# A decoder layer on one core: other queues for three early loads, a second bank for one early product, and two Pool sequences moved by two places and one

## The chip, the core and the metric

The kernel runs on one core of one Trainium2 chip. Five engines matter: TensorE (PE in the profile, its weight loads PEld), VectorE (DVE), ScalarE (ACT), GpSimd (POOL) and SyncE (SP). SP, ACT and POOL can issue DMAs; the profile calls their issuing sides SPq, ACTq and POOLq, and the queues of packets q1 (SP's), q10 (ACT's) and q0 (POOL's). The metric is the device time of one execution in microseconds; less is better. Before the change the median of three runs is 2976.89 us (2976.18 to 2977.85).

## The reference

One decoder layer in float32 over 32 x 64 = 2048 token rows of 512 features. Only the first stage is touched by the change:

```python
q = (x @ wq.T).reshape(b, l, NH, HD)          # 32 heads of 128
k = (x @ wk.T).reshape(b, l, NKV, HD)         # 8 key heads
v = (x @ wv.T).reshape(b, l, NKV, HD)
q, k = apply_rope(q, ...), apply_rope(k, ...)
k_full = concatenate([k_cache[block_idx].reshape(-1, NKV, HD), k[0]])   # 512 cached rows + 64 new
v_full = concatenate([v_cache[block_idx].reshape(-1, NKV, HD), v[0]])
attn = softmax(q @ k_full.T / sqrt(HD))
x = layernorm(x + (attn @ v_full) @ wo.T)
```

After it come cross attention over a second input of the same size, a feed-forward part with eight low-rank experts, and a layer norm after each. They are the same before and after.

## The kernel before, in words

**Tiling.** The 2048 rows are four token blocks of 512 (`NTB`), the 32 query heads are eight groups of four (`g`), each group with its own key head. A unit `n` is one head of one token block: 128 units, four to a block `b`, 16 to a group. In unit `n` PE computes scores (`scores`, L865 to L897), DVE takes the row maximum, ACT the exponentials, DVE turns the weights with a 32x32 transpose, SP moves them with sixteen DMAs (`move`, L933) into `pT`, and PE multiplies them with the values two units later (`values`, L954). PE fills the rest of a unit with products of the query projection for the next block and of the output projection for earlier ones.

**Products.** A 512x512x512 projection is done as seven half-size products (a Strassen-Winograd scheme). `Product.mul` (L374) is one of them: eight matmuls into one PSUM bank. The operands are quarters of the weights and tokens, and sums and differences of quarters. For the first block the query product numbered 1 uses `wq0[1]` and token quarter `q[0,0]`; number 2 uses `wq0[2]` and `q[1,0]`; number 5 uses `wq0[5]`, which is first `wq0[5] + wq0[4]` made by DVE (L1215), and `t[1]` (L1213); number 6 uses `wq0[6]` (L1217) and `t[2]` (L1216). `Queries.step(1)` (L405) writes product 1 to bank `x` and lets ACT copy it to the query tile (L409). `step(2)` accumulates product 2 onto the same bank `x`, so it must come behind that copy, and ACT copies the sum (L413).

**The order of the start** (L718 to L1261) is written by hand for all five engines. SP issues the block indices, three token quarters and weight quarter `wq0[5]`, the rotary tables `cs` and `sn` (L736), the key and value weights of group 0 (`load_group(0, nc.sync)`, L1191, issued at L761), four small vectors, the tokens of block 1 (L116) and four quarters of the output weights. ACT issues three weight quarters and the fourth token quarter `q[1,1]`. POOL writes `off_i` (L742), gathers four times 128 cached key rows (L772), copies the 64 new tokens out of the token quarters (`x128`, L1209), helps with the rotation of the cached keys (`rotate`, L795), and gathers the values. DVE makes operands, rotates the keys in two halves (L1218, L1220), prepares a scale `nrm2` (L1221 to L1224) and adds products up (L1237, L1238, L1246). PE does products 1, 2, 5, 6 of block 0, the new keys and values (`new_keys`, L818: eight matmuls with `wk`, eight with `wv`), the transposes of the rotated keys (`cached_keys`, L842, into the bank `s0`, one half of a scores tile called `startbank`), product 3, and then the first scores.

HW-issued DMAs (SP's and ACT's together) share eight completion semaphores in turn, so the ninth such DMA is issued only when the first has landed; POOL's DMAs have eight of their own. That is why an issue on SP can wait for an older load of SP or ACT.

**Tokens' sums.** Later blocks use a deeper scheme whose token operands are prepared once per token block by POOL: `token_leaves(tb)` (L1078) is a list of 20 steps with places 0 to 19: four loads of 256 KB from `xD` (places 0 to 3, two DMAs each, L1089 and L1090), sums (L1094) and stores to DRAM (L1098). A place is a quarter of a unit: place `p` runs at `n = 1 + p // 4`, quarter `p % 4` (`leaf`, L1407). The line `place += (16, 36, 54, 72)[tb]` (L1273) gives the start of the four sequences. All four use one tile `tq`. At each place without a store POOL also issues one held-back load (`spread`).

Of the kernel before, what the change touches and what calls it, by code (L numbers as in the profile page):

```python
# [9 lines left out]
F32 = mybir.dt.float32  # L10
I32 = mybir.dt.int32
AF = mybir.ActivationFunctionType
ALU = mybir.AluOpType
# [3 lines left out]
P = 128  # L17
# [35 lines left out]
def decoder_layer(  # L53
# [32 lines left out]
    nc = tc.nc  # L86
# [45 lines left out]
    special = {}  # L132

    def bank(shape, name, tag=None):
        if tag in special:
            v = special[tag]
            return v.rearrange("p (a b) -> p a b", a=shape[1])
        return psum[-1].tile(shape, F32, tag=tag or "ps", name=name)
# [105 lines left out]
    def quarter(i, j):  # L244

        return slice(2 * i, 2 * i + 2), slice(j * HF, (j + 1) * HF)
# [20 lines left out]
    def load_quarter(dst, src, i, j, queue=nc.sync):  # L267
        r = slice(i * HF, (i + 1) * HF)
        queue.dma_start(
            out=dst, in_=src[r, j * HF : (j + 1) * HF].rearrange("(c p) n -> p c n", p=P)  # L270
        )
# [48 lines left out]
    def load_right_first(src, name, queue=nc.sync, held=None):  # L320
        w = {}
        load_some(src, name, w, ((1, (0, 0)), (2, (1, 0))), queue, held)
        return w
# [384 lines left out]
    with ExitStack() as ph:  # L708
# [3 lines left out]
        sc = ph.enter_context(tc.tile_pool(name="sc", bufs=2, space=PSUM))  # L712
# [10 lines left out]
        NKT = NSEL // P  # L723
# [4 lines left out]
        q = {(i, j): xTs[0][:, quarter(i, j)[0], quarter(i, j)[1]]  # L728
             for i in range(2) for j in range(2)}
        for i, j, n, (k, m) in ((0, 0, 1, (0, 0)), (1, 0, 2, (1, 0)), (0, 1, 5, (0, 1)), (1, 1, 4, (1, 1))):  # L730
            load_quarter(q[i, j], xT_in, i, j, (nc.sync, nc.scalar)[i and j])
            load_quarter(wq0[n], wqT[:, : REP * HD], k, m, (nc.scalar, nc.sync)[n == 5])
        cs = kc.tile([P, HD // 2], F32, name="cs")
        sn = kc.tile([P, HD // 2], F32, name="sn")
# [6 lines left out]
        for i in range(P // BLOCK):  # L741
            nc.gpsimd.iota(  # L742
                off_i[i * BLOCK : (i + 1) * BLOCK, :], pattern=[[0, 1]], base=0,
                channel_multiplier=1,
            )
        off = kc.tile([P, 1], F32, name="off")
        nc.vector.tensor_copy(off, off_i)
        nc.vector.tensor_scalar(off, off, float(NKV), None, ALU.mult)
# [8 lines left out]
        def load_group(g, queue=nc.scalar):  # L757
            ws = []
            for tag, src in (("wk", wkT), ("wv", wvT)):
                w = kv.tile([P, NC, HD], F32, tag=tag, name=f"{tag}{g}", bufs=1)  # L760
                load = lambda w=w, src=src: queue.dma_start(  # L761
                    out=w, in_=src[:, g * HD : (g + 1) * HD].rearrange("(c p) n -> p c n", p=P)
                )
                if g == 0:
                    load()
                else:
                    spread.append(load)
                ws.append(w)
            wkv_cur[g] = ws
# [25 lines left out]
        def rotate(g, t0=0, t1=NKT):  # L795


            kn = kn_cur[g][:, t0:t1, :].rearrange("p t (d two) -> p t d two", two=2)
            k4 = kr_cur[g][:, t0:t1, :].rearrange("p t (d two) -> p t d two", two=2)
            shape = [P, t1 - t0, HD // 2]  # L800
            c3 = cs[:, None, :].to_broadcast(shape)
            s3 = sn[:, None, :].to_broadcast(shape)
            tmp = kv.tile(shape, F32, tag="tmp", name=f"kt{g}_{t0}", bufs=1)
            tmq = kv.tile(shape, F32, tag="tmq", name=f"kq{g}_{t0}", bufs=1)
            e, o = kn[:, :, :, 0], kn[:, :, :, 1]
            nc.gpsimd.tensor_tensor(k4[:, :, :, 1], o, c3, ALU.mult)
            nc.vector.tensor_tensor(tmq, e, s3, ALU.mult)
            nc.vector.tensor_tensor(k4[:, :, :, 0], e, c3, ALU.mult)
            nc.vector.tensor_tensor(tmp, o, s3, ALU.mult)
            nc.gpsimd.tensor_tensor(k4[:, :, :, 1], k4[:, :, :, 1], tmq, ALU.subtract)  # L810
            nc.vector.tensor_tensor(k4[:, :, :, 0], k4[:, :, :, 0], tmp, ALU.add)
# [6 lines left out]
        def new_keys(g):  # L818

            wk, wv = wkv_cur.pop(g)
            kTs[g] = kv.tile([P, NKEY], F32, tag="kT", name=f"kT{g}")
            new = bank([P, 1, TB], f"new{g}", "po1")[:, 0, :]
            pk, pv = new[:, :SEQ], new[:, P : 2 * P]
            for c in range(NC):
                nc.tensor.matmul(
                    pk, wk[:, c, :], x64[:, c, :], start=(c == 0), stop=(c == NC - 1),
                    skip_group_check=True,
                )  # L830
            for c in range(NC):
                nc.tensor.matmul(
                    pv, x128[:, c, :], wv[:, c, :],
                    start=False, stop=(c == NC - 1), skip_group_check=True,
                )
            nc.scalar.activation(
                kTs[g].rearrange("p (s b k) -> p s b k", s=2, k=SQ)[:, :, SHARED, :],
                pk.rearrange("p (s k) -> p s k", s=2), AF.Copy, scale=nrm2,
            )
            nc.scalar.copy(vs[g][:, NKT, :], pv)  # L840
# [148 lines left out]
        def columns(g):  # L989
            return slice(g * REP * HD, (g + 1) * REP * HD)  # L990

        def start_queries(b, tags):
            g, tb, _ = units[b * REP]
            qTs[b] = big.tile([P, REP, TB], F32, tag="qT", name=f"qT{g}_{tb}", bufs=2)
            qrs[b] = Queries(wq_cur[g], tok.pop(b), qTs[b], f"q{g}_{tb}", tags)
# [192 lines left out]
                    for v, d in ((1, d1), (2, d5), (0, d7)):  # L1188
                        g.tensor_tensor(q[:, v, :, :], q[:, v, :, :], d, add)  # L1189

        load_group(0, nc.sync)  # L1191
        cs2 = kc.tile([P, 1], F32, name="cs2")
        sn2 = kc.tile([P, 1], F32, name="sn2")
        for dst, src in ((cs2, cos2), (sn2, sin2)):
# [4 lines left out]
        xTs[1] = token_room(1, "xT1")  # L1199
        load_features(xTs[1], xT_in, 1)  # L1200
        wo_cur[0] = load_right_first(woT[columns(0), :], "wo0")
        special["s0"] = sc.tile([P, 2, 512], F32, tag="sc", name="startbank")[:, 0, :]

        sub = ALU.subtract
        t = {i: txs[:, i - 1, :, :] for i in range(1, 5)}
# [11 lines left out]
        nc.vector.tensor_tensor(wq0[6], wq0[5], wq0[1], sub)  # L1217
        rotate(0, 0, NKT // 2)  # L1218
        nc.vector.tensor_tensor(wq0[3], wq0[2], wq0[6], sub)
        rotate(0, NKT // 2, NKT)  # L1220
        nc.vector.tensor_tensor(nrm2, cs2, cs2, ALU.mult)  # L1221
        nc.vector.tensor_tensor(sn2, sn2, sn2, ALU.mult)
        nc.vector.tensor_tensor(nrm2, nrm2, sn2, ALU.add)
        nc.vector.tensor_scalar(nrm2, nrm2, SCALE, None, ALU.mult)  # L1224
        wq_cur[0] = wq0
        tok[0] = {1: q[0, 0], 2: q[1, 0], 3: q[1, 1], 4: t[4], 5: t[1], 6: t[2], 7: t[3]}
        start_queries(0, {"x": "q", "y": "w", "z": "po0"})


        first = qrs[0]  # L1230
        c = first.c
        first.step(1)
        first.step(2)
        z = first.mul("z", 5, True)
        y = first.mul("y", 6, True)
        new_keys(0)
        nc.vector.tensor_tensor(c[1, 1], z, c[1, 0], ALU.add)  # L1237
        nc.vector.tensor_tensor(c[0, 1], y, c[1, 0], ALU.add)  # L1238
        nc.vector.tensor_tensor(t[3], q[1, 1], q[0, 1], sub)
        for j in range(NKT):  # L1240
# [29 lines left out]
        leaves, full = {}, set()  # L1270
        for tb in range(NTB):
            for place, part in token_leaves(tb):
                place += (16, 36, 54, 72)[tb]  # L1273
                leaves.setdefault(place, []).append(part)
                if part.__name__ == "store":
                    full.add(place)
# [3 lines left out]
        for n in range(N):  # L1280
# [6 lines left out]
            if 0 < n <= PER:  # L1287
                b2, j = divmod(n - 1, TPB)
# [246 lines left out]
    with ExitStack() as ph:  # L1535
# [39 lines left out]
        def run(todo, count=None):  # L1575
            for _ in range(len(todo) if count is None else min(count, len(todo))):
                todo.pop(0)()
# [37 lines left out]
        with ExitStack() as st:  # L1615
# [8 lines left out]
            def add_bias(tb, j):  # L1624
                a = acc[tb][:, j, :]
                nc.vector.tensor_tensor(a, a, bo, ALU.add)
# [11 lines left out]
            def place(step, todo):  # L1638

                while step in fill:  # L1640
                    step += 1
                fill[step] = todo
                return step + 1
# [14 lines left out]
            for k, tb in enumerate((1, 2, 3, 0)):  # L1658
                stats, (head, *pieces) = layernorm_parts(tb, "a", by_act=True)
                i = place(17 * k, lambda stats=stats: run(stats, 2))  # L1660
                i = place(i, lambda stats=stats: run(stats))
                i = place(i + 1, head)
# [14 lines left out]
            i = 0  # L1677
            for tb, last in zip((1, 2, 3, 0), turned_at):
                i = max(i, last + 2)
                for j in range(TPB):  # L1680
                    while i in fill or i - 1 in fill and i + 1 in fill:
                        i += 1
                    i = place(i, lambda tb=tb, j=j: add_bias(tb, j)) + 1
# [62 lines left out]
        sc = ph.enter_context(tc.tile_pool(name="xsc", bufs=2, space=PSUM, reuse_waits="tile"))  # L1746
# [519 lines left out]
```

## Time and profile before

| what | value |
|---|---|
| median of three runs | 2976.89 us (2976.18 to 2977.85) |
| profiled execution, its own time | 2975.92 us |
| span of that execution | 2974.1 us |
| PE busy | 2953.5 us (99%) |
| DVE, ACT, POOL busy | 1907.9, 1481.7, 1699.0 us |
| PE's first matmul | 5.52 us |
| first product of block 0 on PE | 5.52 to 9.27 us |
| second product | 9.94 to 13.5 us |
| third product | from 13.52 us |
| first scores | 20.96 us |

All times are from the start of the span. The program is one long chain on PE; what lies outside of PE counts only where PE waits. In the timeline an entry reads: start, duration, engine, line, operation, output <- inputs, count, and in brackets the idle time before it with what ended it.

### The profile page before, as it was taken

The page shows a single profiled execution, that of the slowest core. Times are in us where ns is not written, and L with a number is a line of the kernel's source. Part 1 is how long each engine was busy: PE and PEld are TensorE (multiplying, and loading weights), DVE is VectorE, ACT ScalarE, POOL GpSimd, SP SyncE. Part 2 cuts the span into 40 slices and gives each one's busy share as a digit, 9 for nine tenths or more (in the row PEclk, how much of TensorE's full clock was granted, in tenths as well). Part 3 has the DMA queues.
Part 4 walks back from the last instruction along what each step waited for, and adds up shares of the span by engine and source line. Part 5 has one row for each costly group of instructions (what it writes and reads, how often), then busy time and mean ns, then how long its engine had stood idle before and what let it go on. Part 6 is the DMA issues. An engine that isn't in the chain of part 4 may idle for free.

```text
span 2974.1 us, 49389 instructions
## 1 busy us (share of the span) xinstructions
PE 2953.5 (99%) x17152; PEld 2336.2 (79%) x17152; DVE 1907.9 (64%) x3568; ACT 1481.7 (50%) x3304; POOL 1699.0 (57%) x1697
## 2 busy tenths in 40 slices
PE   9999999999999999999999999999999999999998
PEld 6677777777777777777777768999999999999965
DVE  6766666666666666666666665636666666666676
ACT  5444455555455455555555552334555555555564
POOL 5666654564564564664663534658577577567532
PEclk9999999999999999999999999999999999999999
DMA  6677656666666666665566554766455445445420
GB/s 171 182 200 196 171 143 157 159 162 158 156 166 157 154 166 157 154 168 154 155 168 156 136 132 147 255 234 214 160 185 184 168 168 194 166 162 184 137 82 36
DMA packets 220454, 487.31 MB, mean 164 GB/s; under 512 B 52912, under 2 KB 88112, under 8 KB 212016
## 3 DMA queue, kind: packets, MB, share of 16 engines
q1 hardware_dynamic: 177872, 341.51, 39.6%
q0 software_dynamic: 40672, 140.68, 16.7%
q8 instruction: 139, 2.28, 0.3%
q10 hardware_dynamic: 1664, 1.97, 0.2%
q14 instruction: 107, 0.88, 0.1%
HBM read 264.27 MB, written 46.66 MB: 105 GB/s over the span
## 4 chain that ended last, share of the span: by engine, by line
PE 96%; DVE 1%; DMA 1%; SPq 1%; ACT 1%; issue 0%; POOL 0%; POOLq 0%; DVEq 0%
PE po L949 17%; PE s L875 16%; PE qd L1168 9%; PE sx L1762 2%; PE pox L1845 2%; PE qx_0x L519 2%; PE qx_1x L519 2%; PE qx_2x L519 2%; PE qx_3x L519 2%; PE wx_3y L380 1%; PE wx_2y L380 1%; PE wx_0y L380 1%; PE w_3y L380 1%; PE w_0y L380 1%; PE w_2y L380 1%; PE wx_1y L380 1%
## 5 line engine op out<-in xcount | busy, mean ns | idle before, releaser
L875 PE MATMUL s<-kT,qT 128*128 128x288 f32 x2048 | 581.3, 408 | 0.0
L888 ACT ACTIVATE p<-s,nmax 128x576 f32<-128x576 f32 x512 | 378.4, 739 | 362.7 <-DVE nmax L882 341.2
L949 PE MATMUL po<-pT,v 128*128 128x512 f32 (+1 forms) x1280 | 549.5, 603 | 4.6 <-DMA pT<-T 4.2
L882 DVE TENSOR_REDUCE nmax<-s 128x1 f32<-128x576 f32 x512 | 384.5, 751 | 249.1 <-PE s L875 244.2
L919 ACT ACTIVATE p<-p,den 128x576 f32<-128x576 f32 x416 | 322.8, 776 | 354.6 <-DVE den L917 352.8
L875 PEld LDWEIGHTS s<-kT,qT 128*128 128x128 f32 x2048 | 371.0, 190 | 107.2 <-issue 33.9
L929 DVE STREAM_TRANSPOSE T<-p 128x576 f32<-128x576 f32 x512 | 395.6, 773 | 45.7 <-ACT p L919 41.0
L1145 POOL DMA_DIRECT2D tq<-tq x336 | 182.8, 547 | 417.2 <-PE qd L1168 403.4
L949 PEld LDWEIGHTS po<-pT,v 128*128 128x128 f32 (+1 forms) x1280 | 204.0, 189 | 191.0 <-issue 175.4
L1168 PEld LDWEIGHTS qd<-tq,wq 128*128 128x128 f32 x1344 | 174.5, 191 | 48.4 <-issue 31.8
L1168 PE MATMUL qd<-tq,wq 128*128 128x128 f32 x1344 | 179.0, 276 | 0.0
L1168 PEld LDWEIGHTS qd<-tq,xT 128*128 128x128 f32 x1008 | 136.3, 191 | 51.9 <-issue 23.0
L1168 PE MATMUL qd<-tq,xT 128*128 128x128 f32 x1008 | 142.1, 277 | 0.0
L1865 ACT ACTIVATE oTx<-pox,bv 128x128 f32<-128x128 f32 x248 | 71.3, 490 | 128.3 <-PE pox L1845 128.3
L917 DVE RECIPROCAL den<-den 128x1 f32<-128x1 f32 x512 | 78.5, 153 | 72.2 <-ACT p L888 70.7
L1189 POOL TENSOR_TENSOR qT<-qT,tx 128x512 f32<-128x512 f32 x72 | 89.2, 1267 | 61.5 <-DVE qT L1177 61.4
L351 POOL TENSOR_TENSOR sox<-oTx,oTx 128x512 f32<-128x512 f32 x31 | 39.3, 1268 | 148.1 <-DVE oTx L1867 144.3
L1794 ACT ACTIVATE exps<-exps,denx 128x64 f32<-128x64 f32 x480 | 121.1, 338 | 0.0
L561 POOL TENSOR_TENSOR qTx<-d_in 128x512 f32<-128x512 f32 x68 | 85.2, 1275 | 34.5 <-ACT d_in L537 26.7
L888 ACT ACTIVATION_READ_ACCUMULATOR p<-s,nmax 128x1 f32 x512 | 99.5, 194 | 0.0
L1175 ACT COPY tx<-qd 128x512 f32<-128x512 f32 x96 | 56.1, 584 | 67.2 <-PE qd L1168 62.3
L561 POOL TENSOR_TENSOR qTx<-d 128x512 f32<-128x512 f32 x60 | 75.1, 1275 | 25.0 <-ACT d L537 23.5
(626 smaller groups left out, 6352.3 us busy)
## 6 DMA issues: line engine op xcount, KB each, us to landing
pT<-T SPq DMA_DIRECT2D x1016, 80.0 KB
pT<-T SPq DMA_DIRECT2D x1008, 64.0 KB
xT<-tl SPq DMA_DIRECT2D x28, 1792.0 KB
tq<-tq POOLq DMA_DIRECT2D x168, 256.0 KB
tlb<-tl SPq DMA_DIRECT2D x28, 1344.0 KB
tq<-tq POOLq DMA_DIRECT2D x168, 192.0 KB
kv_room<-kv SPq DMA_DIRECT2D x32, 512.0 KB
pTx<-Tx SPq DMA_DIRECT2D x256, 64.0 KB
```

The lines of the kernel that those rows point to most:

```text
L380: nc.tensor.matmul(self.banks[b][:, m, :], self.left[i][:, k, m * P : (m + 1) * P], self.right[i][:, k, :], start=(first and m + k == 0), ...
L519: nc.tensor.matmul(o[:, j, :], self.left[s][:, j, LEFT[i], :], self.right[s][:, j, RIGHT[i], :], start=(first and j == 0), stop=(j == len( ...
L561: nc.gpsimd.tensor_tensor(self.q[:, :, i, :, v, :], x.rearrange("p (o u) n -> p o u n", o=2), y.rearrange("p (o u) n -> p o u n", o=2), AL ...
L875: nc.tensor.matmul(s[:, a, :HALF], query_block(n, i), kTs[g][:, a * HALF : (a + 1) * HALF], start=True, stop=True,)
L882: nc.vector.tensor_reduce(nmax, s[:, :, :HALF], AX.XY, ALU.max, negate=True)
L888: nc.scalar.activation(p.rearrange("q (a k) -> q a k", a=2), s[:, :, :HALF], AF.Exp, bias=nmax, accum_out=den,)
L919: nc.scalar.activation(p, p, AF.Copy, scale=den)
L929: nc.vector.transpose(Ts[n][:, :, i, :], ps_.pop((n, i)).rearrange("q (b k) -> q b k", k=SQ))
L949: nc.tensor.matmul(pos[n].rearrange("d (a q) -> d a q", a=NQD), vs[units[n][0]][rows, v, :], pTs[n // 2][rows, :, chunk, :], skip_group_ch ...
L1145: nc.gpsimd.dma_start(out=tq[:, r, : 4 - s, :], in_=tq_all[b % NTB][:, r, 4 * s : 4 + 3 * s, :],)
L1168: nc.tensor.matmul(o[:, j, :], wdeep[s][:, j, LEFT[i], :], tq[:, RIGHT[i], j, :], start=(first and j == 0), stop=(j == js - 1), skip_group ...
L1794: nc.scalar.activation(e[:, k, :], e[:, k, :], AF.Copy, scale=den[:, k : k + 1])
```

## The change

1. The token quarter `q[1,1]` is no longer issued by ACT between two weight quarters; POOL issues it behind `off_i`, ahead of the key gathers.
2. The key and value weights of group 0 are no longer issued by SP behind the rotary tables; ACT issues them behind its copy of product 1.
3. Product 2 has a PSUM bank of its own, the second half of `startbank` (`s1`), and no longer accumulates onto bank `x`. ACT's copy of the sum is gone; DVE adds bank `s1` and the copy of product 1 instead.
4. The rotation of the second half of the cached keys is done by DVE and POOL behind the four `nrm2` operations, in program order behind `new_keys`.
5. The token sums of block 1 start at place 38 instead of 36, those of block 2 at place 55 instead of 54.

```diff
         for i, j, n, (k, m) in ((0, 0, 1, (0, 0)), (1, 0, 2, (1, 0)), (0, 1, 5, (0, 1)), (1, 1, 4, (1, 1))):
-            load_quarter(q[i, j], xT_in, i, j, (nc.sync, nc.scalar)[i and j])
+            if (i, j) != (1, 1):
+                load_quarter(q[i, j], xT_in, i, j)
             load_quarter(wq0[n], wqT[:, : REP * HD], k, m, (nc.scalar, nc.sync)[n == 5])
...
                 channel_multiplier=1,
             )
+        load_quarter(q[1, 1], xT_in, 1, 1, nc.gpsimd)
         off = kc.tile([P, 1], F32, name="off")
...
-        load_group(0, nc.sync)
         cs2 = kc.tile([P, 1], F32, name="cs2")
...
-        special["s0"] = sc.tile([P, 2, 512], F32, tag="sc", name="startbank")[:, 0, :]
+        startbank = sc.tile([P, 2, 512], F32, tag="sc", name="startbank")
+        special["s0"], special["s1"] = startbank[:, 0, :], startbank[:, 1, :]
...
         rotate(0, 0, NKT // 2)
         nc.vector.tensor_tensor(wq0[3], wq0[2], wq0[6], sub)
-        rotate(0, NKT // 2, NKT)
         nc.vector.tensor_tensor(nrm2, cs2, cs2, ALU.mult)
...
-        start_queries(0, {"x": "q", "y": "w", "z": "po0"})
+        start_queries(0, {"x": "q", "y": "w", "z": "po0", "2": "s1"})
...
         first.step(1)
-        first.step(2)
+        load_group(0, nc.scalar)
+        second = first.mul("2", 2, True)
         z = first.mul("z", 5, True)
         y = first.mul("y", 6, True)
         new_keys(0)
+        rotate(0, NKT // 2, NKT)
         nc.vector.tensor_tensor(c[1, 1], z, c[1, 0], ALU.add)
+        nc.vector.tensor_tensor(c[0, 0], second, c[1, 0], ALU.add)
         nc.vector.tensor_tensor(c[0, 1], y, c[1, 0], ALU.add)
...
-                place += (16, 36, 54, 72)[tb]
+                place += (16, 38, 55, 72)[tb]
```

## The prediction, made before the result was known

> **What bounds the kernel now.** I read the page first, then PE's waits over the whole span, then chain, timeline and waits of the first 26 us, because the change lies there but for one line.
>
> ```profile
> span 2974.1 us, 49389 instructions
> PE 2953.5 (99%) x17152; PEld 2336.2 (79%) x17152; DVE 1907.9 (64%) x3568; ACT 1481.7 (50%) x3304; POOL 1699.0 (57%) x1697
> ```
>
> PE is busy 2953.5 of 2974.1 us. The 20.6 us left are all that better waiting can win.
>
> ```profile
> engine line waited for: us in total, times, longest us
> PE q_0x L380 <- DMA xT<-in_xT: 5.5, 1, 5.5
> PE po L949 <- DMA pT<-T: 4.2, 5, 1.3
> PE q_0x L380 <- ACT qT L409: 0.7, 1, 0.7
> ```
>
> PE's waits: 5.5 us for the first tokens, 4.2 us in five waits for moved weights, and 0.7 us between products 1 and 2, the wait for ACT's copy that the change removes.
>
> ```profile
> 9.94 3.76 PE L380 MATMUL q_0x<-xT,wq 128*128 128x256 f32 x8 [0.68 <-ACT qT L409]
> ...
> 11.68 0.69 DVE L1214 TENSOR_TENSOR wq<-wq 128x512 f32<-128x512 f32 x1 [1.11 <-DMA wq<-in_wqT]
> 12.40 0.92 DVE L1215 TENSOR_TENSOR wq<-wq 128x512 f32<-128x512 f32 x1
> ...
> 13.37 1.67 PEld L380 LDWEIGHTS q_0z<-tx,wq 128*128 128x128 f32 x8 [0.37 <-DVE wq L1215]
> 13.52 1.92 PE L380 MATMUL q_0z<-tx,wq 128*128 128x256 f32 x8
> ```
>
> This timeline is the core of the case. The third product (q_0z) needs L1215, which comes behind L1214, which waited until 11.68 for a weight load. Its own weights were loaded only 0.37 us after PEld was free. So behind the 0.68 us stands a second limit: landing + 0.69 + 0.92 + hand-overs = 13.52 - 11.68 = 1.84 us.
>
> ```profile
> L380 PE MATMUL q_0x<-xT,wq x16: 614/632/797, 5.5 to 13.1; 128*128 128x256 f32 x16
> ...
> L380 PE MATMUL q_0z<-tx,wq x8: 379/379/412, 13.5 to 15.1; 128*128 128x256 f32 x8
> ```
>
> The same shape takes 632 ns until 13.1 us and 379 ns from 13.5 us, though the clock column shows 1.00 throughout. The first eight start (3.75 - 0.63)/7 = 0.446 us apart.
>
> ```profile
> SPq L761 <- DMA xT<-in_xT: 1.9, 1, 1.9
> SPq L1198 <- DMA wq<-in_wqT: 1.0, 1, 1.0
> ...
> SPq L1195 <- DMA xT<-in_xT: 0.5, 1, 0.5
> SPq L269 <- DMA wv<-in_wvT: 0.5, 1, 0.5
> SPq L269 <- DMA wk<-in_wkT: 0.4, 1, 0.4
> ```
>
> SP's issues wait for older landings, so they date them: the third token quarter 9.80 (L1195's second issue), wq0[5] 11.67 (second L1198), wk 13.48, wv 14.39 (L269).
>
> ```profile
> 8.00:9.00 1.00, 1.00 (x3) 0.45 (x2) 0.00 (x0) 0.00 (x0) 0.27 (x1) 1.00 1.16 340
> 9.00:10.00 1.00, 0.33 (x2) 0.06 (x1) 0.12 (x1) 0.58 (x1) 0.06 (x1) 1.00 0.62 156
> 10.00:11.00 1.00, 1.00 (x3) 0.82 (x4) 0.57 (x1) 0.00 (x0) 1.00 (x2) 1.00 0.40 99
> ```
>
> Last columns: DMA share and GB/s. The DMA engines are full to 9 us and 40% busy in 10:11, while wq0[5] has still not landed.
>
> **The change part by part** (sum against the profiled execution's 2975.92 us: the span plus 1.8; the median of the runs is 0.97 above it).
>
> *Product 2 in its own bank.* The 0.68 us wait goes. Product 2 then runs 8 x 0.446 = 3.57 us from 5.52 + 8 x 0.446 = 9.09, ending at 12.66 instead of 13.52: at most 0.86 earlier at this pace. Its tokens were there by 8.32 (SP's L761 stopped waiting). Late next is L1215: if wq0[5] still lands at 11.67, product 5 starts at 13.5 and nothing is won. So the gain hangs on that landing.
> The page "TensorE: Matmul & The Clock Gate" of the Trainium skill (Part 1) says that the array runs at half clock until one free-running window of about 3.4 us has been busy. By it, an estimate, a gapless start ends the slow stretch between 8.9 and 12.3, and product 2 could end up to 1.8 us sooner than 12.66.
>
> *When wq0[5] lands.* It stays fourth on SP's queue. ACT's queue has a quarter (256 KB) less, POOL's one more. Ends: straight behind the third token quarter at 9.80, 1.87 us earlier; or the moved quarter delays it by its own 256 KB at the 340 GB/s of the full stretch, 0.8 us later. I take the half of the first, 0.94 earlier, since in 10:11 the engines are 60% idle and only a tail of the load is out. Product 5 then could start at 12.58; PE is free at 12.66: **gain 0.86 us**. Ends: -0.8, and +1.87 if product 2 ran at the full pace of q_0z, (1.92 - 0.38)/7 = 0.22 us a matmul, and so ended at 10.85.
> The page "DMA: Bandwidth & Descriptors" (Issuing engines are not separate DMA queues) speaks against it: all issuers run on the same 16 engines, and spreading saves sequencer time alone. By that rule this gain is 0. The trace moved equal shares of both queues from 3.3 to 7.5 us, which fits, but its 40% at 10:11 says that something other than bandwidth ends the load.
>
> *The token quarter on POOL.* One issue, 0.55 us (POOL's L122 rows, same size), at about 1.95 in the 1.42 us that POOL waits for L785: free. Gathers, issued from 3.35, showed no packet of q0 before 7.5, so POOL's loads start late; the quarter is wanted at 9.94 by L1209 (its reader new_keys: 17.0) and 13.24 by L1216. The gathers stand behind it: 256 KB at 340 to 99 GB/s is 0.8 to 2.6 us. L806 got its keys at 12.31, DVE's L807 used them at 14.45: cover 1.7 us. Cost 0, end 0.9.
>
> *Key and value weights on ACT.* Two issues of 0.38 us behind the copy that ends at 9.88, plus a wait for a semaphore. Behind them on ACT the next work is at 18.99: free. SP loses both issues and 2.2 us of waits, so block 1's tokens (issued 12.04) start earlier. The loads reach the DMAs at 10 to 12 instead of 6.02 and 8.32, into the idle stretch. PE wants wk at 16.8 and wv at 17.8. Earliest wv: 10.3 + 1.7 (index load: issue 0.75, used 2.41) + 512 KB at 340 = 13.5. Latest: shared to the end with 2 MB of SP's loads, 2.6 MB at 350 from 11.7: 19.2. I take the middle, 16.4: no cost; end +1.4, and 1.8 more if the issue must await wq0[5] (9.88 to 11.67).
>
> *DVE.* A 0.69 us addition replaces ACT's 0.58 us copy. DVE runs without a break from 11.68 to 20.54 and then waits 1.29 us for product 3 (L1246): covered. The second rotation (16.39 to 17.55) comes behind four operations that take 0.65, ending 0.65 later; the transposes' weights load at 18.68: 0.5 us of cover left. Product 3 reuses the bank read by L1237, which stays in place.
>
> *Token sums.* Same instructions and bytes. POOL was held until 143.70 by ACT's copies (9.79 us idle), then issued block 1's loads between 148.7 and 158.2; two places later only puts two held-back loads ahead. One wait of 0.9 us for moved weights stands at 163.3. It may go (-0.9) or become the longest of its kind (+0.4), and the same once at block 2 (+1.3, none there now). Block 2's first load now shares a place with block 1's last store from that quarter, so POOL waits there longer (3.4 us was the longest such wait); behind it are loads for a unit or more later. I take 0.
>
> *Sum.* 2975.92 - 0.86 = 2975.06. The median stood 0.97 above the profile; the three runs spread 1.67 us, and one product at slow instead of full pace costs 8 x (0.446 - 0.22) = 1.8 us, so that excess may be slow products, which would now fall before PE's wait. I keep half of it, 0.48: **2975.5 us**.
>
> **The rivals.**
> 1. *The load hides it.* wq0[5] lands at 11.67 as before; PE only waits elsewhere. 2975.92 plus up to 0.97: 2976.4. For it: the same queue place. Against: ACT's queue is shorter.
> 2. *Slower: PE waits for wv in new_keys.* It decides from the point where wv lands after 17.8 less the gain, 16.9. At 19.2 the stall is 2.3, net +1.4: 2977.8 with half the excess; with the semaphore wait 2979.6. For it: SP's 2 MB come earlier. Against: the idle stretch.
> 3. *Key gathers late.* DVE's rotation waits 0.9; the gain is eaten: 2976.4.
> 4. *Something outside this sum*, such as pT moves falling out of step, either sign, over 6 us.
>
> **How the numbers follow.** Forecast 0.40, rivals 0.18, 0.22, 0.08, the rest 0.12. The forecast's own range is 2974.2 (0.86, and 0.9 at 163 us) to 2976.4. The range for all reaches from 2975.92 - 1.87 - 0.9 = 2973.1, put at 2973.0, to the dear end of rival 2 with 0.4 for a longer wait at 163 us, 2980.0, and leaves out most of the rest. A measurement of this kernel tells about 0.2% (6 us) from no change. All named cases lie within it: 0.88. The rest gives faster 0.04 and slower 0.08, since PE has only 20.6 us to win.
>
> **What would show it.** Right: q_0x without the 0.7 us wait; L1214 starting near 10.7; q_0z near 12.7; no PE wait at new; first scores near 20.1. Wrong: L1214 at 11.7 (rival 1); PE waiting for wv (2); L807 waiting for kn (3); new waits at L949 after 143 us (4).

## The result, and the profile after

The changed kernel takes 2981.39 us (median of 22 runs, 2978.82 to 2983.46), the kernel before 2976.57 us in the same series (22 runs, 2973.05 to 2980.10). The ratio is 1.0017, 95% interval 1.0010 to 1.0023. The change costs 4.8 us, where a time 1.4 us under the first median had been forecast; the time lies 1.4 us above the range. The profiled execution of after took 2982.57 us, 1.2 us above its median.

The page's span and busy times of after:

```profile
span 2980.8 us, 49393 instructions
PE 2955.2 (99%) x17152; PEld 2338.4 (78%) x17152; DVE 1902.6 (64%) x3569; ACT 1482.3 (50%) x3303; POOL 1701.6 (57%) x1698
```

The span grew by 6.7 us and PE's busy time by 1.7. So some 5 us net are new waiting, and the rest is TensorE doing the same work more slowly (net as well: product 2 runs faster, what stands behind the new wait slower). PE's waits of after (who waits for what: us in total, times, longest):

```profile
engine line waited for: us in total, times, longest us
PE q_0x L380 <- DMA xT<-in_xT: 5.2, 1, 5.2
PE new L829 <- DMA wk<-in_wkT: 4.5, 1, 4.5
...
PE q_0z L380 <- DVE wq L1217: 0.9, 1, 0.9
...
PE new L834 <- DMA wv<-in_wvT: 0.2, 1, 0.2
```

The 0.7 us wait for ACT's copy is gone, as the change meant. A wait of 0.9 us stands at product 5 instead, and one of 4.5 us at the new keys: TensorE has nothing to do until the key weights land. The timeline of after (start, duration, instruction, the idle time before it in brackets) shows how late they were sent for:

```profile
8.73 2.23 PE L380 MATMUL startbank<-xT,wq 128*128 128x256 f32 x8
9.18 0.43 SPq L116 DMA_DIRECT2D xT<-in_xT  x1
...
10.08 0.38 ACTq L763 DMA_DIRECT2D wk<-in_wkT  x1
10.15 0.94 DVE L1216 TENSOR_TENSOR wq<-wq 128x512 f32<-128x512 f32 x1 [0.21 <-DMA wq<-in_wqT]
10.50 1.47 ACTq L763 DMA_DIRECT2D wv<-in_wvT  x1
11.87 1.99 PE L380 MATMUL q_0z<-tx,wq 128*128 128x256 f32 x8 [0.91 <-DVE wq L1217]
...
20.05 1.94 PE L829 MATMUL new<-x,wk 128*128 128x64 f32 x8 [4.46 <-DMA wk<-in_wkT]
22.18 2.05 PE L834 MATMUL new<-wv,x 128*128 128x128 f32 x8 [0.18 <-DMA wv<-in_wvT]
...
24.87 2.68 PE L380 MATMUL q_0z<-xT,wq 128*128 128x256 f32 x8
27.39 1.13 PE L877 MATMUL s<-kT,qT 128*128 128x288 f32 x4
```

The lines of before for the same steps:

```profile
12.04 0.43 SPq L116 DMA_DIRECT2D xT<-in_xT  x1
...
17.01 1.00 PE L827 MATMUL new<-x,wk 128*128 128x64 f32 x8
...
17.84 1.11 PE L832 MATMUL new<-wv,x 128*128 128x128 f32 x8
...
20.96 1.13 PE L875 MATMUL s<-kT,qT 128*128 128x288 f32 x4
```

SP sends off the 1 MB of block 1's tokens at 9.18; ACT follows with wk at 10.08 and wv at 10.50. Product 5 starts at 11.87 (before: 13.52), so the start itself is faster. Then the key weights let TensorE start only at 20.05. What follows runs slowly as well: the products with wk take 1.94 us (before 1.00) and those with wv 2.05 (before 1.11). The table by stretches of after tells why (the columns are PE, PEld, DVE, ACT and POOL busy, PE's granted clock, the DMA engines' busy share, GB/s):

```profile
14.00:16.00 2.00, 1.59 (x8) 1.06 (x6) 1.93 (x8) 0.00 (x0) 0.68 (x2) 1.00 1.09 362
16.00:18.00 2.00, 0.00 (x0) 0.00 (x0) 1.97 (x7) 0.00 (x0) 1.60 (x2) 1.00 1.12 327
18.00:20.00 2.00, 0.00 (x0) 0.00 (x0) 1.87 (x4) 0.00 (x0) 1.49 (x2) 0.91 0.97 304
20.00:22.00 2.00, 1.94 (x8) 1.78 (x8) 0.00 (x0) 0.00 (x0) 1.64 (x2) 0.50 0.78 198
...
24.00:26.00 2.00, 2.00 (x9) 1.82 (x8) 0.00 (x0) 1.13 (x4) 0.00 (x0) 0.50 0.00 0
26.00:28.00 2.00, 2.00 (x9) 1.66 (x9) 0.40 (x1) 0.00 (x0) 0.00 (x0) 0.88 0.00 0
```

The clock falls to one half at 19.65, 0.4 us before the products with wk start, and stays there until 26.47. In 14:20 the DMA engines are full: the weights were not waiting for an idle machine, they stood among other transfers.

So the loss can be read off the start of unit 0's scores, 20.96 us before and 27.39 after. TensorE was ready for the new keys at 17.01 before and at 20.05 - 4.46 = 15.59 after:

- start, products 1, 2, 5 and 6: 15.59 - 17.01 = **-1.42**
- waits for wk and wv: 4.46 + 0.18 = **+4.64**
- the same work from the new keys to the scores, without the second wait: (27.39 - 20.05 - 0.18) - (20.96 - 17.01) = 7.16 - 3.95 = **+3.21**, at the half clock for all but the last 0.9 us
- sum +6.43.

From there on the two traces stay within half a microsecond of that distance: unit 4 starts 6.75 us later than before, unit 17 6.30, unit 120 6.25, and the end is 6.64 later. All of the loss arises in 12 us. (The medians differ by 4.8 and not by 6.6, because this execution of after stands 1.2 above its median and the execution of before 0.65 below the median of its 22 runs.)

### The profile page after: what moved, and what is told of

Its sections match the earlier page's. It is cut to its first block, busy times and chain, and to the rows that moved or that the text cites. A ratio compares the mean times of both kernels' runs of the same rounds, so it can differ in the third digit from the quotient of the medians.

```text
span 2980.8 us, 49393 instructions
## 1 busy us (share of the span) xinstructions
PE 2955.2 (99%) x17152; PEld 2338.4 (78%) x17152; DVE 1902.6 (64%) x3569; ACT 1482.3 (50%) x3303; POOL 1701.6 (57%) x1698
## 3 DMA queue, kind: packets, MB, share of 16 engines
q8 instruction: 139, 2.28, 0.3%
## 4 chain that ended last, share of the span: by engine, by line
PE 94%; DVE 2%; DMA 1%; SPq 1%; POOL 1%; ACT 1%; issue 0%; POOLq 0%; ACTq 0%; DVEq 0%
PE po L951 17%; PE s L877 17%; PE qd L1170 9%; PE sx L1766 2%; PE pox L1849 2%; PE qx_1x L519 2%; PE qx_0x L519 2%; PE qx_2x L519 2%; PE qx_3x L519 2%; PE wx_3y L380 1%; PE wx_2y L380 1%; PE wx_0y L380 1%; PE w_2y L380 1%; PE w_3y L380 1%; PE w_1y L380 1%; PE w_0y L380 1%
## 5 line engine op out<-in xcount | busy, mean ns | idle before, releaser
L351 POOL TENSOR_TENSOR so<-oT,oT 128x512 f32<-128x512 f32 x32 | 40.8, 1274 | 84.7 <-ACT oT L974 84.5
```

## The experiments

Each run is told by the start of unit 0's scores in its profile, since single executions of one kernel differ by several us (22 runs of the kernel before spread over 7 us), and by its median beside that of the kernel before in the same series. Theory from here on: *the loads of the key and value weights were sent off behind 1 MB of other loads, and the wait for them takes the clock down*.

**The weights back on SP, in their old place.** (e1) The rest of the change stays.

```
+        load_group(0, nc.sync)
         cs2 = kc.tile([P, 1], F32, name="cs2")
...
-        load_group(0, nc.scalar)
```

> The changed kernel with one part undone: wk and wv are issued by SP in their old place; all else is as changed. Theory A (the late wk and wv cost the 6.4 us at the first scores: 4.5 + 0.2 us of waiting at new_keys and about 2.5 us of slow matmuls after the wait, less 1.65 us won at product 5): no wait at new_keys, PE's clock never falls back, first scores at 19.3 to 20.0 instead of 27.39, time 1 to 1.6 us below the kernel before, about 2975.3. Rival B (the token quarter on POOL's queue or the moved rotation holds the chain as well): the wait moves to the transposes or to product 3 and first scores stay above 21.5, time 1 us or more above the kernel before.

Measured: 2975.10 us (11 runs; kernel before 2975.34; ratio 0.9997, 0.9988 to 1.0006). There is no wait at the new keys; they start at 15.44, with wv at 16.28. So the moved loads are the whole loss. But the scores start at 20.56 and not before 20, since the gain runs into a new wait. Timeline of this run:

```profile
16.58 0.43 DVE L813 TENSOR_TENSOR kr<-kr,kt 128x128 f32<-128x128 f32 x1
16.94 0.68 DVE L1240 TENSOR_TENSOR qT<-q_0z,qT 128x512 f32<-128x512 f32 x1
17.54 0.67 DVE L1241 TENSOR_TENSOR qT<-startbank,qT 128x512 f32<-128x512 f32 x1
...
18.36 0.63 PE L848 MATMUL startbank<-ident,kr 128*128 128x128 f32 x4 [0.97 <-issue]
```

The transposes of the cached keys write the first half of startbank. The rotated keys were ready at 17.01, but the transposes start 0.15 us after L1241 ended (18.21), the addition that reads product 2 from the *second* half. A run below tests whether it is that.

**The loads alone.** (e2) The kernel before, with the loads of wk and wv moved to ACT behind its copy and nothing else changed.

```
-        load_group(0, nc.sync)
...
         first.step(1)
+        load_group(0, nc.scalar)
         first.step(2)
```

> The kernel before with this part alone: wk and wv issued by ACT behind its copy of product 1. Theory A: PE waits 3 us or more at new_keys, the clock falls back if the wait passes about 3.4 us, first scores at 24 to 27.5, time 3 to 6 us above the kernel before. Rival B (the loads are late only because the token quarter went to POOL): wk lands before 17.0, no wait at new_keys, time within 1 us of the kernel before.

Measured: 2981.55 us (10 runs; ratio 1.0017, 1.0008 to 1.0027), as slow as the whole change. Timeline of this run:

```profile
19.84 1.29 PE L827 MATMUL new<-x,wk 128*128 128x64 f32 x8 [2.77 <-DMA wk<-in_wkT]
22.09 2.04 PE L832 MATMUL new<-wv,x 128*128 128x128 f32 x8 [0.97 <-issue]
```

TensorE is ready at 17.07 here and waits 2.77 + 0.97 us (for the 0.97 the profile names no releaser; that it is wv is read from the last packet of ACT's queue, which starts 0.63 us before those products, as it does 0.64 us before them in after), then loses 3.04 us at the half clock (27.80 - 19.84 - 0.97 = 6.99 against 3.95). The scores start at 27.80, +6.84. The token quarter on GpSimd isn't needed for the loss. The whole change waits longer (4.64 us), and there TensorE is ready 1.48 us sooner.

**Issued late, but by SP and ahead of block 1's tokens.** (e3)

```
             nc.sync.dma_start(out=dst, in_=src)
+        load_group(0, nc.sync)
         xTs[1] = token_room(1, "xT1")
         load_features(xTs[1], xT_in, 1)
...
-        load_group(0, nc.scalar)
```

> The changed kernel with wk and wv issued by SP, as late as ACT did (behind bv, about 9.2 us), but ahead of block 1's tokens. If the competition with SP's 2 MB (tokens of block 1 and output weights) delays them: with that stood behind them they land by 13.5 to 15, no wait at new_keys, first scores near 19.5 to 20. If the late issue itself is enough: they land after 17, PE waits 1.5 us or more at new_keys, first scores above 22.

Measured: 2975.21 us (10 runs; ratio 0.9996, 0.9987 to 1.0006). Timeline of this run:

```profile
15.82 1.00 PE L829 MATMUL new<-x,wk 128*128 128x64 f32 x8
```

The new keys start without a wait, the scores at 20.80. A later issue alone does no harm; it is what stands ahead of it, or ACT's queue. The next two runs tell these two apart.

**ACT's late loads, with block 1's tokens behind them.** (e5) The tokens of block 1 and the first output weights are issued by ACT too, behind wv.

```
-        load_features(xTs[1], xT_in, 1)
-        wo_cur[0] = load_right_first(woT[columns(0), :], "wo0")
...
         load_group(0, nc.scalar)
+        load_features(xTs[1], xT_in, 1, nc.scalar)
+        wo_cur[0] = load_right_first(woT[columns(0), :], "wo0", nc.scalar)
```

> The changed kernel with one difference: the tokens of block 1 (1 MB) and the first two quarters of the output weights, which SP issues from 9.18 us on in the changed kernel, are issued by ACT behind wk and wv. So wk and wv are still issued late (about 10.1 and 10.5 us) and still by ACT, but nothing from SP stands beside them. Theory A (what is in flight ahead of them: wk's first packets moved only when 1 MB of tokens was half through): wk lands before 15.7 us and wv before 17, no wait of more than 0.5 us at the new keys, the granted clock stays at 1.00 to 27 us, scores of unit 0 begin at 20 to 21 us against 27.4, and the time is 2974.5 to 2976.5. Theory B (ACT's queue is itself late or slow, whatever stands beside it): the wait for wk stays at 3 us or more, new keys begin after 18.7 us, scores of unit 0 begin after 25 us, and the time is 2979 to 2982.

Measured: 2975.49 us (10 runs; kernel before 2976.24; ratio 0.9999, 0.9989 to 1.0008). Timeline of this run:

```profile
9.21 1.64 SPq L269 DMA_DIRECT2D wo<-in_woT  x2
...
10.11 0.38 ACTq L763 DMA_DIRECT2D wk<-in_wkT  x1
...
11.78 0.37 ACTq L763 DMA_DIRECT2D wv<-in_wvT  x1
12.19 0.52 ACTq L116 DMA_DIRECT2D xT<-in_xT  x1
...
15.54 1.08 PE L829 MATMUL new<-x,wk 128*128 128x64 f32 x8
17.14 1.13 PE L834 MATMUL new<-wv,x 128*128 128x128 f32 x8 [0.52 <-DMA wv<-in_wvT]
```

Same engine, same queue, same time of issue (10.11 against 10.08), and wk is there by 15.54. Only wv, issued 1.3 us later than in after, makes TensorE wait 0.52. ACT's queue isn't the harm. One thing differs from what the expectation says: two other quarters of the output weights (0.5 MB) are still sent off by SP, at 9.21 and so ahead of wk. wk moves beside them (in 12:14 SP's queue moved 0.31 MB and ACT's 0.20). So 0.5 MB on SP's queue ahead of wk did not make TensorE wait for wk, where the tokens' 1 MB did.

**The opposite: SP issues them, behind block 1's tokens.** (e10)

```
         load_features(xTs[1], xT_in, 1)
+        load_group(0, nc.sync)
...
-        load_group(0, nc.scalar)
```

> The changed kernel with wk and wv issued by SP, directly behind the tokens of block 1 (1 MB) and ahead of the output weights. Theory A (what counts is what is in flight ahead of them, not the queue that issues them): the tokens need about 3 us at the 350 GB/s that were moved then, so wk lands at 16 to 19 us and wv 0.7 us later, PE waits 0.5 to 3.5 us at the new keys (changed kernel 4.46), scores of unit 0 begin at 21.5 to 26 us, time 2976 to 2980. Theory B (ACT's queue, which takes turns with SP's, is the harm): no wait over 0.5 us at the new keys, scores of unit 0 by 21 us, time 2975 to 2976.

Measured: 2978.61 us (10 runs; kernel before 2976.37; ratio 1.0009, 0.9999 to 1.0018). Timeline, then the stretches of this run:

```profile
9.77 0.43 SPq L116 DMA_DIRECT2D xT<-in_xT  x1
10.24 0.51 SPq L763 DMA_DIRECT2D wk<-in_wkT  x1
...
19.06 1.94 PE L829 MATMUL new<-x,wk 128*128 128x64 f32 x8 [3.28 <-DMA wk<-in_wkT]
```

```profile
16.00:18.00 2.00, 0.00 (x0) 0.00 (x0) 1.97 (x6) 0.00 (x0) 1.51 (x2) 1.00 1.15 319
18.00:20.00 2.00, 0.94 (x5) 0.97 (x5) 2.00 (x4) 0.00 (x0) 1.39 (x3) 0.52 1.11 344
```

The wait is back, 3.28 us, and the clock falls again. With SP issuing ahead of the tokens there is no wait, behind them 3.28; with ACT issuing ahead of the tokens there is 0.52 for wv, behind them 4.64. So the place against the 1 MB decides, and who issues is second. The scores start at 25.90 (+4.94: -1.23 at the start, +3.28, +2.89 by the clock).

**The wait filled with work.** (e4) The changed kernel, with ten extra products of no use (each stands as two matmuls in the trace) written, ahead of the new keys, into a part of their bank that is not read; TensorE then works while wk is on its way.

> The changed kernel with ten more matmuls (4.3 us at full pace) on PE ahead of new_keys, written to an unused part of its bank; their result is not used. Theory A with a clock part: PE is busy through the wait, the granted clock stays 1.00 to the end, the matmuls of new_keys, the transposes and product 3 take 275, 272 and 379 ns as in the kernel before instead of the slow ones, and first scores come about 2.5 us before 27.39, near 24.9; time about 2.5 us below the changed kernel. If the slow matmuls were not from the wait: still slow, first scores at 27 or later.

Measured: 2980.90 us (10 runs; kernel before 2975.34; ratio 1.0016, 1.0007 to 1.0025). Timeline of this run:

```profile
15.69 4.48 PE L829 MATMUL new<-xT,wq 128*128 128x256 f32 x20
20.00 1.00 PE L834 MATMUL new<-x,wk 128*128 128x64 f32 x8
20.84 1.11 PE L839 MATMUL new<-wv,x 128*128 128x128 f32 x8
...
23.95 1.13 PE L882 MATMUL s<-kT,qT 128*128 128x288 f32 x4
```

The new keys start at 20.00, as late as in after (20.05), but take 1.00 and 1.11 us, as before. From there to the scores it is 3.95 us, exactly the figure before, where after needs 7.16 without its wait for wv. That shows the +3.21 to be a consequence of TensorE's standing still, not of the late weights or busy queues. The median, however, gains nothing sure by it: 0.5 us, where 2.5 were expected. In this execution, 2.6 us go around the start of unit 6, where TensorE waits 2.24 us for moved weights (after: 1.37) and the clock drops once more from 81.4 to 84.8. Why that stall is longer here stays open.

**Product 2's addition behind the transposes** (e6), on top of the first experiment.

```
-        nc.vector.tensor_tensor(c[0, 0], second, c[1, 0], ALU.add)
...
         cached_keys(0, "s0")
+        nc.vector.tensor_tensor(c[0, 0], second, c[1, 0], ALU.add)
```

> The changed kernel with wk and wv issued by SP in their old place (the run e1_loads_by_sp, in which the transposes of the cached keys begin at 18.36 us after a wait of 0.97 us and the scores of unit 0 at 20.56), and one line moved: VectorE's addition of product 2 to c[0,0], which reads the second half of startbank, stands behind the transposes, which write the first half, and not ahead of them. Theory A (the transposes wait for that addition, which ended at 18.21 us in e1, since both use the tile startbank): the transposes begin at 17.4 to 17.6 us, right behind the products with wv, the scores of unit 0 at 19.5 to 20.0, and the median falls by about 0.9 us, to 2974.0 to 2974.6. Theory B (they wait for the second rotation of the keys, which ended at 17.01 us and whose keys landed at 14.8): nothing moves, transposes at 18.3, scores of unit 0 at 20.5, 2975.1. In both, ratio to the kernel before 0.998 to 1.000.

Measured: 2975.04 us (11 runs; kernel before 2976.24; ratio 0.9996, 0.9987 to 1.0005). Timeline of this run:

```profile
14.96 0.29 DVE L809 TENSOR_TENSOR kq<-kn,sn 128x128 f32<-128x128 f32 x1 [2.25 <-DMA kn<-in_k_cache,row]
...
16.91 0.38 PE L848 MATMUL startbank<-ident,kr 128*128 128x128 f32 x2
19.05 0.41 PE L848 MATMUL startbank<-ident,kr 128*128 128x128 f32 x2 [1.76 <-DVE kr L813]
19.56 3.48 PE L380 MATMUL q_0z<-xT,wq 128*128 128x256 f32 x8
```

The first two transposes now start right behind the products with wv, so in the first experiment it was the addition that held them (theory A in its mechanism). The other two wait 1.76 us for the second rotation, because in this execution the gathered keys landed at 14.96 (13.08 in the first experiment). The 0.9 us of the forecast are lost to that, and the stall takes the clock down here too (q_0z 3.48 us instead of 1.89), and the scores start at 22.83 and not by 20.0. The median is that of the first experiment (2975.10) within the noise.

**The second rotation directly behind the first** (e9), on top of that.

```
         rotate(0, 0, NKT // 2)
+        rotate(0, NKT // 2, NKT)
         nc.vector.tensor_tensor(wq0[3], wq0[2], wq0[6], sub)
...
-        rotate(0, NKT // 2, NKT)
```

> The kernel of e6_sum_behind_transposes (wk and wv on SP in their old place, the addition of product 2 behind the transposes) with the second rotation of the cached keys directly behind the first, ahead of wq0[3] and the four small operations for the norm; in e6 it began 1.34 us after the first rotation's end, and the last two transposes waited for it 1.76 us. Theory A (late gathered keys and the place of the second rotation are what is left at the transposes): no wait over 0.5 us at the transposes where the first rotation starts by 13.5 us, and one of 0.3 to 0.9 us where it starts at 15 us as in e6; scores of unit 0 begin at 19.5 to 20.2 us (or 21.5 where the keys are late and the clock falls back), median 2973.5 to 2974.8, ratio to the kernel before 0.9985 to 0.9998. Theory B (the gain at the start is given back at the transposed weights of unit 6, as in e3, e4 and e6, where a stall of 2.2 us stands there): a stall of 2 us or more in unit 6 and median 2974.8 to 2976.

Measured: 2974.51 us (11 runs, 2972.86 to 2975.97; kernel before 2976.37, 2973.70 to 2979.46; ratio 0.9994, 0.9985 to 1.0003). No wait at the transposes (the first rotation starts at 13.81), scores at 19.98. It is the lowest median of the study and far below the changed kernel, but the interval doesn't part it from the kernel before.

**The single parts on the kernel before.** First (e11) the own bank for product 2, with its addition behind the transposes:

```
-        special["s0"] = sc.tile([P, 2, 512], F32, tag="sc", name="startbank")[:, 0, :]
+        startbank = sc.tile([P, 2, 512], F32, tag="sc", name="startbank")
+        special["s0"], special["s1"] = startbank[:, 0, :], startbank[:, 1, :]
...
-        first.step(2)
+        second = first.mul("2", 2, True)
```

> The kernel before with the third part of the change alone: product 2 in its own bank, its addition to c[0,0] on VectorE behind the transposes. Theory A (the wait of 0.68 us for ACT's copy goes, and with it the half clock on product 2, since TensorE no longer stands still between products 1 and 2): the granted clock rises before 10.5 us (kernel before: 13.55), product 2 takes about 2.1 us and not 3.8, products 5 and 6 wait up to 1 us for VectorE, scores of unit 0 begin at 19.3 to 20.6 us (before 20.96), median 2975.0 to 2976.3. Theory B (the wait only moves to product 5 and the transposes): scores of unit 0 at 20.7 to 21.2 us, median 2976.2 to 2977.

Measured: 2974.98 us (10 runs; kernel before 2976.37; ratio 0.9998, 0.9988 to 1.0007). Timeline of this run:

```profile
8.63 3.06 PE L380 MATMUL startbank<-xT,wq 128*128 128x256 f32 x8
12.58 1.99 PE L380 MATMUL q_0z<-tx,wq 128*128 128x256 f32 x8 [0.88 <-DVE wq L1216]
```

Scores at 20.09, 0.86 earlier, as theory A says; the clock rose at 11.0, later than its 10.5, so product 2 took 3.06 us rather than 2.1. The wait moves to product 5 (0.88 us for VectorE, which waited for wq0[5]).

The token quarter on GpSimd alone (e8):

> The kernel before with the first part of the change alone: GpSimd issues the fourth quarter of the tokens, and ACT does not. Theory A (the loads of the key and value weights behind ACT's copy are the whole loss): no wait at the new keys, the scores of unit 0 begin between 20.3 and 21.8 us (before: 20.96), and the time is 2975 to 2978. Theory B (the quarter on GpSimd pushes the gathers of keys back and this costs at the transposes): the second gather begins 0.9 us later, transposes wait 0.4 us or more for the rotated keys, and the scores of unit 0 begin after 21.3 us.

Measured: 2975.68 us (8 runs; kernel before 2976.24; ratio 0.9998, 0.9988 to 1.0008). Scores at 21.37 (before 20.96), no wait at the new keys or the transposes, the first rotation at 12.95 (before 14.45): theory A (21.37 lies in the ranges of both; that nothing waits decides). The gathers are not pushed back (the second is issued at 4.83, before 4.81).

The places of the tokens' sums alone (e7):

```
-                place += (16, 36, 54, 72)[tb]
+                place += (16, 38, 55, 72)[tb]
```

> The kernel before with the fourth part of the change alone: the places of the sums of tokens are 16, 38, 55, 72 and not 16, 36, 54, 72. Theory A (the later places take TensorE's waits of 1 us for transposed weights in units 7 to 17 away): the start of unit 17 is 0.5 to 1.5 us earlier than in the kernel before, the start of unit 6 within 0.1, and the median 2974.9 to 2976.1. Theory B (the place does nothing, and what the changed kernel won between units 7 and 17 comes from the moved start): the start of unit 17 within 0.2 us, 2976.2 to 2976.9.

Measured: 2976.43 us (11 runs; kernel before 2976.24; ratio 1.0001, 0.9992 to 1.0010). In its profile the waits at 89, 163 and 233 us of the kernel before are gone (the one at 76 is longer, 2.1 us against 1.3), and unit 17 starts 2.79 us earlier. But 0.98 of that stands before unit 0 already, which this edit doesn't touch, and the run above, which has the old places, gains 1.6 us between units 6 and 17 too. These waits come and go from one execution to the next, and the median says theory B. Whether the places do anything is not settled; it is less than the measurement tells.

Put together, by where wk and wv stand:

| kernel | wk and wv | waits for them, us | scores of unit 0, us | median (before in the series) |
|---|---|---|---|---|
| before | SP, ahead of the tokens | 0 | 20.96 | 2976.57 |
| e1 | SP, ahead | 0 | 20.56 | 2975.10 (2975.34) |
| e3 | SP, late, ahead | 0 | 20.80 | 2975.21 (2975.34) |
| e5 | ACT, late, ahead | 0.52 | 20.93 | 2975.49 (2976.24) |
| e10 | SP, late, behind | 3.28 | 25.90 | 2978.61 (2976.37) |
| after | ACT, late, beside and behind | 4.64 | 27.39 | 2981.39 (2976.57) |
| e2 | ACT, late, beside and behind | 3.74 | 27.80 | 2981.55 (2975.34) |

## Why the prediction was wrong

**The step that failed is *Key and value weights on ACT*.** It let wk and wv land "into the idle stretch", took the middle of 13.5 and 19.2, 16.4, and set the cost to nothing. wk let TensorE start at 20.05 and wv at 22.18. Three things were wrong in it.

- The middle was no reading: no row stood for it. The row that would have told stood in the step itself: SP's issue of block 1's tokens moves forward once SP no longer issues wk and wv and waits for them. It went from 12.04 to 9.18, and so *ahead* of ACT's issue at 10.08. The idle stretch was then filled by 1 MB that is wanted later than wk: in before block 1's tokens are first used at 23.90 (GpSimd) and 24.62 (TensorE's q_1x), wk at 17.01. The DMA table of after for 12:14, when wk had been out for 2 us (queue, packets, MB, share of the engines' time; q1 is SP's queue and q10 ACT's):

```profile
q1 hardware_dynamic: 408, 0.56, 79.1%
...
q10 hardware_dynamic: 1, 0.00, 0.1%
```

  In 10:12 ACT's queue moved no packet at all, though the DMA engines were only 48% busy: wk's first packet came at 13.92, 3.84 us after its issue (in e5, with the tokens behind it, 1.5 us after). So full engines are not the whole delay; what kept the first packet back for so long no run here shows. In the next stretch, 14:16, ACT's queue gets its share:

```profile
q1 hardware_dynamic: 272, 0.42, 56.9%
q10 hardware_dynamic: 583, 0.29, 50.8%
```

  The weights go in packets of 0.29 MB / 583 = 500 bytes. Per byte they take 50.8/0.29 against 56.9/0.42, 1.3 times the engines' time of SP's.
- The latest bound was too low as well. It shared 2.6 MB at 350 GB/s from 11.7. In fact 0.60 + 0.72 + 0.65 + 0.61 + 0.40 = 2.98 MB passed between 12 and 22 us, at 298 GB/s, and the load isn't done with its mean packet but with its last: by 18 us 0.47 MB of ACT's 0.5 had moved, and the last 100 packets (61 in 18:20, 39 in 20:22) took until wv was whole at 22.
- The stall was priced as its own length. It costs another 3.21 us, because the clock falls. My text drew on the Trainium skill's "TensorE: Matmul & The Clock Gate" (Part 1) for the start alone and did not apply its other half, that the clock falls again after an idle window, to rival 2, which was the rival with a stall. (Its 2.3 us would have filled no window of 3.4 us; the runs show, below, that 2.24 can be enough.)

**Rival 2 is what happened**, in the right place (the new keys) with the wrong weight: already wk was late, the wait was 4.64 and not 2.3, and its dear end of 2979.6 lies under the median. Its chance of 0.22 against 0.40 for the forecast rested on the idle stretch, which the change itself filled.

**Product 2 in its own bank: right in the wait, and its number met by luck.** The 0.7 us wait goes, and the wait moves to product 5, as said (0.88 us alone, 0.91 in after). The part alone brings the scores 0.86 us forward and lets product 5 start at 12.58, the very figures of the forecast, but not by its working: product 2 ended at 11.70 and not at 12.66, as it started 0.46 us sooner and the clock rose on the way (at 11.0, and at 9.41 in after, inside the 8.9 to 12.3 of the estimate); and wq0[5] was first used at 11.11, 0.57 us before the 11.68 of before, although that run leaves the quarter on ACT.

**When wq0[5] lands: right in size.** I took 0.94 us earlier. VectorE's first operation on it (which in some runs waits for something else last) starts at 11.68, 11.16, 10.77 and 11.11 us in the four profiles with the quarter on ACT (mean 11.18), and at 10.15, 10.30, 10.79, 10.46, 10.18, 9.89, 10.04, 11.00 and 10.32 in the nine with the quarter on GpSimd (mean 10.35): 0.83 earlier. Part of the 1.65 us by which product 5 came forward in after is chance of this kind. The Trainium skill's "DMA: Bandwidth & Descriptors" (Issuing engines are not separate DMA queues) says that all issuers end on the same 16 engines. My working from it put this gain at 0, against my own figure; the runs show 0.83, and not why. For the loads of wk and wv, though, the sentence is the one that counts: ACT's queue offered no road of its own past SP's 1 MB (0.29 of the 0.72 MB moved in 14:16 were ACT's, none before 13.92).

**The token quarter on POOL: right.** Cost 0; the gathers were not pushed back.

**DVE: the cover was there, the danger named was the wrong one.** The forecast left the second rotation 0.5 us of cover. In the first experiment the rotation was in time and the addition of product 2, which I had called covered, held the transposes for 0.97 us: VectorE is indeed busy without a break there, but I had only asked whether it delays VectorE, not who waits behind it in the same tile. In after this is hidden under the wait for wk.

**Token sums: 0 taken**, and nothing that the runs can tell from 0.

**The sum.** With the step put right, 2975.92 - 1.42 + 4.64 + 3.21 = 2982.35 for an execution like the one profiled (measured 2982.57). The three terms are read from that same execution, so this is a check of the account and no second forecast. The 0.48 us that the forecast kept for slow products is shown by no run: over 22 runs the median before stands 0.65 above its profiled execution, and that of after 1.18 below its own. Nor do the medians show the gain that was forecast: with wk and wv back in their place (e1) the kernel is level with the one before, 0.9988 to 1.0006.

## What to carry to other kernels

When an issue is taken off a queue, everything behind it on that queue moves forward; look at what now goes off ahead of the moved load, and count its bytes. A load that TensorE wants soon belongs ahead of a large one that is wanted later; which engine issues it matters less. Price a stall of TensorE by its length and by the slow stretch that may follow (here 4.64 and 3.21 us), and ask of each operation moved onto an engine also who else uses the tile that it reads.

## What the hardware showed

The clock falls and rises on a grid. In after it rises at 9.41 us, falls at 19.65 and rises at 26.47: 3 x 3.413 and 5 x 3.413 us after the first rise. In the other profiles, too, the slow stretches inside the program last 3.41 us (e3, e4, e6) or 6.83 (e2, e10, after). This agrees with the free-running window of about 3.4 us that the Trainium skill states in "TensorE: Matmul & The Clock Gate" (Part 1). The page has the clock fall after an idle window; here a window that was idle in part was enough, and the measurement decides. Laid on this grid, the windows after which the clock fell held 1.86 (e6), 2.24 (e3 and e4), 2.28 (e10), 2.69 (e2) and 3.41 us (after) without a matmul. Over the thirteen profiles, the ends of the programs included, the clock fell after every window that held 2.11 us or more and after none that held 1.84 or less; with 1.86 it fell in e6 and not at the end of e10. So a long wait can be harmless where an edge of the grid cuts it: one of 3.01 us in e5 (from 75.55, also ahead of unit 6) lay across the edge at 77.34, with 1.79 and 1.22 us in the two windows, and the clock stayed at 1.00. The ends of matmuls are modelled, so no exact threshold follows between 1.84 and 2.11.

Whether the slow stretch lasts one window or two goes with the first window in it: with 0.59 (after), 0.97 (e2) and 1.00 us (e10) without a matmul there, the clock came back only after the next one, which was full; with none there (e3, e4, e6) it came back at its end.

The 0.68 us gap between products 1 and 2 may have a price beyond its length. In three of the four profiles with the gap the clock rose at 13.6 to 14.2 us (9.8 in the fourth) and product 2 took 3.8 us; in the nine without it the clock rose at 9.1 to 11.2 and product 2 took 2.0 to 3.3 us. In the three the gap lay inside one window of the grid (6.73 to 10.14 in before), and the clock rose at the end of the next; in the fourth (e7) 0.62 us of it lay in the window that ended at 9.84, and the clock rose there all the same. So the runs don't show that the gap alone decides. The clock column of the tables by stretches says 1.00 for these first microseconds as well; only the durations (634 ns against 379 for one matmul) show that they were slow.
